# A fused graph and transformer layer on one core: seven blocks of normed tokens go through DRAM and are turned by VectorE

## The chip, the cores and the metric

The kernel runs on one core of a Trainium2 chip. A core has five engines that work side by side, each with its own list of instructions in a fixed order: TensorE (PE in the profile; its loading of weights is PEld), VectorE (DVE), ScalarE (ACT), GpSimd (POOL) and SyncE (SP), which here issues DMAs. They wait for each other through semaphores. Tiles lie in SBUF, a memory of 128 partitions; TensorE writes its products into PSUM; inputs, outputs and scratch tensors lie in DRAM and are moved by the core's 16 DMA engines. The metric is the device time of the whole kernel in microseconds, the median of several runs.

## The reference

4096 tokens of 256 values pass through one layer. First a graph part, then a transformer block on its normed result:

```python
x = x + gnn(layernorm(x), adj, neigh_W, lin_W)
x = x + ffn(layernorm(x))

def gnn(f, adj, neigh_W, lin_W):
    h = adj @ (f @ neigh_W.T) / (adj.sum(axis=1, keepdims=True) + 1.0)
    return concatenate([f, h], axis=-1) @ lin_W.T
```

`adj` is 4096 x 4096. The `ffn` is causal attention (4 heads for queries, 2 for keys and values, of 64 values, with rotary embedding) and a mixture of 8 experts of which each token uses 2. All is in float32.

## The kernel before

The tokens are cut into eight blocks of 512 (`NB`), a block into four tiles of 128 (`TB`). The kernel has three stages: the graph part with the making of queries, keys and values (to about 514 us), attention, and the experts. The change lies in the first.

The first stage makes eight passes, one for each block `b` of output tokens (`aggregate`, L510). A pass makes eight steps, one for each block `jb` of input tokens. A step multiplies one tile of adjacency of 1 MB, `a`, with the normed tokens `g[jb]`. It does so by seven products of halves instead of eight (Strassen's scheme), for which VectorE first makes four sums of parts of `a` (`halve`, L478: four instructions, L489 to L492, one of which writes into `a` itself). In TensorE's list a step has 28 instructions at L532. The order is written by hand: `aggregate` calls `halve` for the next step first, then the products, then a list of other work after the fourth of the seven products (`steps[jb]`), more at the step's end (`steps[jb, "end"]`), and then the load of the adjacency tile that is three steps ahead (`load`, L268). Three buffers hold adjacency, so this load can only start when the step's own tile has been read for the last time. All loads are issued on SP's queue, in the order of the program: a DMA that waits on SP holds back those behind it.

The other work of pass `b` is the making of queries, keys and values for block `b - 1` (`qkv`, L562), as one list for each step: in step 1 `scales` (statistics of the tokens) and `turn_tables` (VectorE turns the rotary tables, which lie along the other axis in DRAM, L311); in step 2 `norm` (VectorE writes the normed tokens `h0` into the buffers of this block's keys and values, L174) and `spread_tables` (three DMAs from SBUF to SBUF, L316); in step 3 `turn` (L582): TensorE turns `h0` so that channels lie on partitions, eight instructions with an identity matrix into PSUM (L431), and ScalarE copies the result to `qT[b]` in two instructions (L433); in step 4 `values_and_logits` (L589, with TensorE's L596) and the keys (`turned_heads`, L608, with TensorE's L612); in step 5 the queries. Rotation reads PSUM on VectorE (L619) and ScalarE (L621), and is ended by GpSimd (L625, L626). Block 7, the last, is not made by `qkv` but in the next stage.

`qT_all` holds the queries of all blocks, 1024 columns each. The columns of block `b + 1` are free while block `b` is being made, except for those of block 7, which hold sums of adjacency in this stage.

Of the kernel before, what the change touches and what calls it, by code (L numbers as in the profile page):

```python
# [9 lines left out]
F32 = mybir.dt.float32  # L10
# [3 lines left out]
ALU = mybir.AluOpType  # L14
# [3 lines left out]
P = 128  # L18
N = 4096
C = 256  # L20
# [46 lines left out]
def fast_kernel(  # L67
# [104 lines left out]
    def normed(dst, b, t, scale):  # L172

        nc.vector.tensor_scalar(  # L174
            dst, res[b][:, t, :], mv[b][:, t, 0:1], scale, op0=ALU.subtract, op1=ALU.mult
        )
# [8 lines left out]
        vv[NB - 1].rearrange("p (r t) c -> p r (t c)", r=2),  # L185
    ]
    m_late = qT_all[:, (NB - 1) * 1024 :][:, 0 : 2 * (C + 1)].rearrange("p (c o) -> p c o", c=2)

    def linear(pool, b, r, banks, m_sb):

# [16 lines left out]
    def ratio(pool, b):  # L207

        r = pool.tile([P, TB, 1], F32, tag="ratio", name=f"ratio_{b}", bufs=1)
        nc.vector.reciprocal(r, both[b])  # L210
        nc.vector.tensor_mul(r, r, rstd[b])
        return r
# [40 lines left out]
    with (  # L253
# [14 lines left out]
        def load(n):  # L268

            if n < NB * NB:  # L270
                blocks[n] = adjs.tile([P, TB, 512], F32, tag="a", name=f"a_{n // NB}_{n % NB}")
                nc.sync.dma_start(blocks[n], adj[n // NB, n % NB])
# [35 lines left out]
        def turn_tables(b):  # L308

            for k in range(2):  # L310
                nc.vector.transpose(tables[b][0:Q, k, :], tables[b][3 * Q :, k, :])  # L311

        def spread_tables(b):

            for n in range(1, 4):
                nc.sync.dma_start(tables[b][n * Q : (n + 1) * Q], tables[b][0:Q])  # L316
# [193 lines left out]
        def aggregate(b, steps):  # L510

            acc = [
                pool.tile([P, 2, 2 * P], F32, tag="acc", name=f"acc_{b}_{k}")
                for k, pool in enumerate((p_acc0, p_acc0, p_acc1, p_acc1))
            ]
            p = {number: acc[bank][:, at, :] for number, (bank, at) in AT.items()}

            u2 = u4 = neighbours[1][:, 0]
            u3 = neighbours[1][:, 1]
            for jb in range(NB):  # L520
                if b:
                    halve(b * NB + jb + 1)
                m = halves_of.pop(b * NB + jb)
                if jb == 0 and b:
                    load_tables(b - 1)
                for i, (number, left, right) in enumerate(
                    BY_BANK if jb in (0, NB - 1) else PRODUCTS
                ):
                    bank, at = AT[number]
                    for k in range(2):  # L530

                        nc.tensor.matmul(  # L532
                            acc[bank][:, at, :], g[jb][:, right, k, :], m[left][:, k, :],
                            start=(jb == 0 and k == 0 and at == 0),
                            stop=(jb == NB - 1 and k == 1),
                            skip_group_check=True,
                        )
                    if i == 3:
                        if jb == NB - 1:
                            nc.scalar.copy(u2, p[1])  # L540
                            nc.vector.tensor_add(neighbours[0][:, 0], u2, p[2])
                            nc.vector.tensor_add(u2, u2, p[6])
                            nc.vector.tensor_add(u3, u2, p[7])
                        for step in steps.get(jb, ()):
                            step()
                for step in steps.get((jb, "end"), ()):
                    step()
                load(b * NB + jb + 3)
            nc.vector.tensor_add(u4, u2, p[5])
            nc.vector.tensor_add(neighbours[1][:, 0], u4, p[3])  # L550
            nc.vector.tensor_sub(neighbours[0][:, 1], u3, p[4])
            nc.vector.tensor_add(neighbours[1][:, 1], u3, p[5])

        def turn_banks(b, r):
            return (
                p_pj.tile([P, 512], F32, tag="pj", name=f"ph_{b}_{r}"),
                p_tr.tile([P, 2, 2, P], F32, tag="tr", name=f"ph_{b}_{r}_1").rearrange(
                    "p c t i -> p (c t i)"
                ),
            )  # L560

        def qkv(b):  # L562

            made = {}

            def scales():
                stats(gx, b)
                var = mv[b][:, :, 1:2]
                power(both[b], var, *BOTH)
                power(rstd[b], var, 1.0, EPS_LN)  # L570

            def norm():

                made["h0"] = [
                    t.rearrange("p (t c) -> p t c", t=2)
                    for t in (kT[b], vv[b].rearrange("p t c -> p (t c)"))
                ]
                for t in range(TB):
                    normed(made["h0"][t // 2][:, t % 2, :], b, t, both[b][:, t])
                made["ratio"] = ratio(gx, b)  # L580

            def turn():  # L582

                made["hT"] = qT[b]
                transposed(
                    lambda t, c: made["h0"][t // 2][:, t % 2, c * P : (c + 1) * P], made["hT"]
                )

            def values_and_logits():  # L589
                for h in range(2):  # L590
                    pj = p_tr.tile([P, 2, 2, P], F32, tag="tr", name=f"pv_{b}_{h}")
                    pj = pj.rearrange("p c t i -> p c (t i)")
                    for i in range(2):
                        at = (2 * h + i) * P
                        for c in range(2):
                            nc.tensor.matmul(  # L596
                                pj[:, i, 0 : NE + P], made["hT"][:, c, at : at + P],
                                wqkv_sb[:, c, QK:], start=(c == 0), stop=(c == 1),
                            )
                    nc.scalar.copy(vv[b][:, 2 * h : 2 * h + 2, :], pj[:, :, NE : NE + P])  # L600
                    for i in range(2):
                        t = 2 * h + i
                        nc.scalar.activation(
                            first_lg[b][:, t, :], pj[:, i, 0:NE], AF.Copy,
                            scale=made["ratio"][:, t],
                        )

            def turned_heads(ms):  # L608
                pjs = [p_pj.tile([P, 512], F32, tag="pj", name=f"pq_{b}_{m}") for m in ms]
                for m, pj in zip(ms, pjs):  # L610
                    for c in range(2):
                        nc.tensor.matmul(  # L612
                            pj, wqkv_sb[:, c, m * P : (m + 1) * P], made["hT"][:, c, :],
                            start=(c == 0), stop=(c == 1),
                        )
                for m, pj in zip(ms, pjs):
                    to = kT[b] if m == 2 else qT[b][:, m, :]
                    rot = gx.tile([P, 512], F32, tag="rot", name=f"rot_{b}_{m}", bufs=1)
                    nc.vector.tensor_mul(to, pj, tables[b][:, 0, :])  # L619
                    for n in range(4):  # L620
                        nc.scalar.activation(  # L621
                            rot[n * Q : (n + 1) * Q, :], pj[(n ^ 1) * Q : ((n ^ 1) + 1) * Q, :],
                            AF.Copy, scale=1.0 if n % 2 else -1.0,
                        )
                    nc.gpsimd.tensor_mul(rot, rot, tables[b][:, 1, :])  # L625
                    nc.gpsimd.tensor_add(to, to, rot)  # L626

            return [
                [scales, lambda: turn_tables(b)], [norm, lambda: spread_tables(b)], [turn],
                [values_and_logits, lambda: turned_heads((2,))], [lambda: turned_heads((0, 1))],  # L630
            ]

# [37 lines left out]
        for b in range(NB):  # L672
            if b:

                steps = {0: behind, (0, "end"): at_end}
                behind = []
                for jb, fs in enumerate(qkv(b - 1)):
                    steps[jb + 1] = fs
            aggregate(b, steps)
            at_end = [lambda b=b: [linear(gx, b, r, turn_banks(b, r), m_sb) for r in range(2)]]  # L680
        nc.scalar.copy(m_late, m_sb)
# [4 lines left out]
    with (  # L686
# [201 lines left out]
            for p in range(2):  # L888
                nc.vector.tensor_mul(ys[b, p], ys[b, p], qT[b][:, p, :])


        def in_order(x):
            return x.rearrange("p (g c d) -> p c g d", g=4, c=2)

        def in_groups(x):
            return x.rearrange("p (c g d) -> p c g d", g=4, c=2)

        def inputs(b):

# [1077 lines left out]
        def step():  # L1977
            for f in next(rest, []):
                f()
# [802 lines left out]
```

## Time and profile before

| What | Number |
|---|---|
| Median of three runs | 1519.27 us (1518.95 to 1519.53) |
| The profiled execution, its own time | 1519.28 us |
| Its span, from the first to the last instruction | 1517.6 us |
| Granted TensorE clock, as a share of full speed | 0.999 |
| TensorE busy | 1504.7 us, 99% of the span |
| VectorE, ScalarE, GpSimd busy | 1071.6, 553.3, 564.8 us |
| One pass of the first stage | 59.70 us |
| One step of 28 products | 6.04 us |
| Adjacency loads, 1 MB each, from issue to landing | 64, median 4.9 us |

The share of busy time is an average over three stages. Where a step's work has to be ready, and what comes last there, is read from the chain of work that ended last and from the engines' timelines. In both, a line shows the start and the length in microseconds, the engine, the line of the kernel and the operation, what it writes and reads, and the count; in square brackets stands the idle time before it and what ended that. In the answers for single lines, the three numbers after the count are the shortest, median and longest duration in nanoseconds.

### The profile page before, as it was taken

How to read it: one execution, taken by the hardware profiler on the slowest of the kernel's cores; microseconds unless marked ns; L12 is line 12 of the kernel's file. 1: busy time of each engine (PE TensorE's matmuls, PEld its weight loads, DVE VectorE, ACT ScalarE, POOL GpSimd, SP SyncE). 2: the span in 40 equal slices, each digit the busy share in tenths (PEclk: the TensorE clock that was granted, in tenths of full speed). 3: DMA queues.
4: the chain of work that ended last, by engine and by line, in shares of the span. 5: the costliest groups of instructions: out<-in, count | busy, mean ns of one | idle time of the engine just before them, and what ended most of it. 6: DMA issues, size and time to landing. Idle time of an engine off the chain costs nothing.

```text
span 1517.6 us, 28636 instructions
## 1 busy us (share of the span) xinstructions
PE 1504.7 (99%) x10795; PEld 1109.5 (73%) x10795; DVE 1071.6 (71%) x2223; ACT 553.3 (36%) x991; POOL 564.8 (37%) x649
## 2 busy tenths in 40 slices
PE   9999999999999999999999999999999999999997
PEld 8888888888888643444444444348899999999996
DVE  7864655655756577778879879795676877777872
ACT  2102021121121356565655655653222344343341
POOL 2102122121220422364564553551523464554542
PEclk9999999999999999999999999999999999999999
DMA  6434544544434100001010111029977898999965
GB/s 243 132 121 149 175 143 131 171 143 149 154 138 152 36 2 16 29 33 52 33 43 31 43 44 31 29 67 330 259 188 214 257 268 243 268 267 247 274 155 134
DMA packets 105774, 212.19 MB, mean 140 GB/s; under 512 B 62394, under 2 KB 82106, under 8 KB 91994
## 3 DMA queue, kind: packets, MB, share of 16 engines
q1 hardware_dynamic: 92090, 192.00, 39.0%
q0 software_dynamic: 12720, 17.47, 6.4%
q8 instruction: 87, 1.43, 0.4%
q10 hardware_dynamic: 816, 0.79, 0.2%
q14 instruction: 61, 0.50, 0.1%
HBM read 184.48 MB, written 27.13 MB: 139 GB/s over the span
## 4 chain that ended last, share of the span: by engine, by line
PE 97%; DMA 1%; DVE 1%; POOL 0%; ACT 0%; issue 0%; SPq 0%; POOLq 0%; DVEq 0%
PE acc L532 25%; PE sc L785 15%; PE h L1793 13%; PE y_first L827 5%; PE y_second L827 5%; PE y_third L827 5%; PE ye_y L1847 4%; PE hA L1610 4%; PE ye_y L1750 3%; PE ye_ms L1750 3%; PE pq L612 2%; PE hD L1610 2%; PE pf L503 2%; PE ph L193 2%; PE po L913 1%; PE hB L1610 1%
## 5 line engine op out<-in xcount | busy, mean ns | idle before, releaser
L785 PE MATMUL sc<-qT_all,kT 64*64 64x512 f32 (+3 forms) x2304 | 282.1, 557 | 0.5 <-ACT pt_all L793 0.3
L532 PE MATMUL acc<-a,g 128*128 128x256 f32 x1024 | 244.0, 379 | 0.0
L532 PEld LDWEIGHTS acc<-a,g 128*128 128x128 f32 x1024 | 193.5, 190 | 31.8 <-issue 6.7
L785 PEld LDWEIGHTS sc<-qT_all,kT 64*64 64x64 f32 x2304 | 91.2, 133 | 128.6 <-issue 109.2
L793 ACT ACTIVATE pt_all<-sc 128x1024 f32<-128x1024 f32 (+3 forms) x157 | 148.8, 955 | 96.7 <-PE sc L785 94.2
L1873 POOL DMA_INDIRECT acc_dram<-y,late x40 | 63.3, 1583 | 176.9 <-ACT y L1862 113.5
L532 PE MATMUL acc<-more_sums,g 128*128 128x256 f32 x512 | 126.3, 379 | 0.0
L813 DVE TENSOR_TENSOR late<-late,pt_all 128x1024 f32<-128x1024 f32 (+3 forms) x91 | 106.8, 1174 | 24.3 <-POOL pt_all L795 9.9
L433 ACT COPY qT_all<-tr 128x512 f32<-128x512 f32 x30 | 16.3, 589 | 259.1 <-PE tr L431 259.1
L625 POOL TENSOR_TENSOR rot<-rot,tables 128x512 f32<-128x512 f32 x21 | 33.9, 1613 | 198.7 <-ACT rot L621 158.5
L532 PEld LDWEIGHTS acc<-more_sums,g 128*128 128x128 f32 x512 | 97.2, 190 | 13.2
L827 PE MATMUL y_first<-pt_all,vv 64*64 64x512 f32 (+3 forms) x448 | 106.6, 554 | 0.0
L1793 PE MATMUL h<-late,qT_all 128*128 128x256 f32 (+1 forms) x616 | 104.0, 327 | 0.2 <-DMA qT_all<-in_w_dram 0.2
L827 PE MATMUL y_second<-pt_all,vv 64*64 64x512 f32 (+3 forms) x436 | 104.2, 555 | 0.0
L1793 PEld LDWEIGHTS h<-late,qT_all 128*128 128x128 f32 x616 | 93.5, 191 | 9.9 <-ACT late L1477 1.1
L1075 POOL DMA_INDIRECT lists<-row,slots x64 | 88.4, 1381 | 17.3 <-issue 14.9
L827 PE MATMUL y_third<-pt_all,vv 64*64 64x512 f32 (+3 forms) x372 | 88.7, 555 | 0.0
L1800 DVE TENSOR_TENSOR late<-si,h 128x256 f32<-128x256 f32 (+2 forms) x87 | 39.4, 466 | 65.0 <-ACT si L1799 46.9
L621 ACT ACTIVATE rot<-pq 32x512 f32<-32x512 f32 x84 | 49.5, 589 | 82.6 <-DVE qT_all L619 43.6
L1799 ACT ACTIVATE si<-h 128x256 f32<-128x256 f32 (+2 forms) x87 | 36.0, 418 | 107.4 <-PE h L1793 98.5
L813 DVE TENSOR_TENSOR sum_all<-sum_all,pt_all 128x1024 f32<-128x1024 f32 (+3 forms) x51 | 56.0, 1098 | 15.8 <-POOL pt_all L795 9.5
L793 ACT ACTIVATE late<-sc 128x1024 f32<-128x1024 f32 (+3 forms) x55 | 50.9, 927 | 41.3 <-PE sc L785 37.9
(493 smaller groups left out, 3337.3 us busy)
## 6 DMA issues: line engine op xcount, KB each, us to landing
a<-in_adj_dram SPq DMA_DIRECT2D x64, 1024.0 KB, 4.9
qT_all<-in_w_dram SPq DMA_DIRECT2D x18, 1408.0 KB, 11.6
pt_all<-in_w_dram SPq DMA_DIRECT2D x16, 1408.0 KB, 10.8
res_all<-in_w_dram SPq DMA_DIRECT2D x17, 768.0 KB, 5.5
pt_all<-in_w_dram SPq DMA_DIRECT2D x16, 768.0 KB, 5.5
res_all<-in_w_dram SPq DMA_DIRECT2D x8, 1408.0 KB
qT_all<-in_w_dram SPq DMA_DIRECT2D x9, 768.0 KB, 5.4
late<-lists SPq DMA_DIRECT2D x96, 64.0 KB, 4.6
```

The lines of the kernel that those rows point to most:

```text
L532: nc.tensor.matmul(acc[bank][:, at, :], g[jb][:, right, k, :], m[left][:, k, :], start=(jb == 0 and k == 0 and at == 0), stop=(jb == NB - ...
L621: nc.scalar.activation(rot[n * Q : (n + 1) * Q, :], pj[(n ^ 1) * Q : ((n ^ 1) + 1) * Q, :], AF.Copy, scale=1.0 if n % 2 else -1.0,)
L785: nc.tensor.matmul(ps[k * HP : (k + 1) * HP, j, :w], kT[sb][hd, i * P + k * HP : i * P + (k + 1) * HP], qT[b][hd, p, off:], start=True, st ...
L793: nc.scalar.activation(pt[:, :, :w], ps[:, :, :w], AF.Exp, scale=HD ** -0.5)
L813: nc.vector.tensor_add(sums[b, p][:, :, off:], before[:, :, off:], pt[:, :, : 512 - off])
L827: nc.tensor.matmul(accs[b, p][k][hd, off:], vv[sb][some, i, hd], pt[some, j, : 512 - off], start=(s == order_of(b)[0]), stop=(s == order_o ...
L1075: put = nc.gpsimd.indirect_dma_start(out=lists[:, :], out_offset=bass.IndirectOffsetOnAxis(ap=chosen[b][:, k, t, :], axis=0), in_=flats[b] ...
L1610: nc.tensor.matmul(bank[:, n, :], m[left][:, c, :], m[right], start=first and n == 0, stop=True, skip_group_check=True,)
L1750: nc.tensor.matmul(p[number], m[left][:, j, :], m[right][:, j, :], start=(n % 4 == 0 and j == 0), stop=(j == 2), skip_group_check=True,)
L1793: nc.tensor.matmul(ps[m % 2][:, m // 2 - q, :], w13_sb[:, c, m * P : (m + 1) * P], xT[:, c, :], start=(c == 0), stop=(c == 1),)
L1847: nc.tensor.matmul(ps[h if last else 0][:, h, :], hT[:, q, cols], w2_sb[:, q, :], start=(q == 0), stop=(q == NF),)
L1873: put = nc.gpsimd.indirect_dma_start(out=(acc_dram if k < NM - LAST else out)[:, :], out_offset=at, in_=y[:, h, :], in_offset=None, comput ...
```

## The change

The seven blocks that `qkv` makes (0 to 6) are no longer turned by TensorE. `norm` writes the four groups of 32 channels of each head half in another order (`in_order`, `in_groups`, which were defined further down and are now above). `leave` stores the normed tokens in a scratch tensor in DRAM, `turning`, of which there are two for alternate blocks. `fetch` reads them back with four DMAs, each of which fills 32 partitions, in runs of 64 values, so that squares of 32 x 32 lie where they belong and only have to be turned in place; the target is `z`, in the columns of the next block in `qT_all`, or in a new tile `last_z` for block 6. `turn` is then two instructions of VectorE, one for each half of the channels.

The places move too. In step 2, `norm` is followed by `leave`; `fetch` stands at the end of step 2, ahead of the load of the adjacency of step 5; `spread_tables`, which followed `norm`, comes after this load, at a new place in the list called "loaded". `turn` moves from the middle of step 3 to its end. Step 3 has nothing in its middle.

```diff
@@ aggregate @@
                 for step in steps.get((jb, "end"), ()):
                     step()
                 load(b * NB + jb + 3)
+                for step in steps.get((jb, "loaded"), ()):
+                    step()
@@ before qkv @@
+        turning = [tc.dram_tile([512, C], F32, name=f"turning{n}") for n in range(2)]
+        last_z = gs.tile([P, 1024], F32, name="last_z")
@@ qkv, with in_order and in_groups @@
+    def in_order(x):
+        return x.rearrange("p (g c d) -> p c g d", g=4, c=2)
+    def in_groups(x):
+        return x.rearrange("p (c g d) -> p c g d", g=4, c=2)
...
                 for t in range(TB):
-                    normed(made["h0"][t // 2][:, t % 2, :], b, t, both[b][:, t])
+                    nc.vector.tensor_scalar(
+                        in_order(made["h0"][t // 2][:, t % 2, :]), in_groups(res[b][:, t, :]),
+                        mv[b][:, t, 0:1], both[b][:, t], op0=ALU.subtract, op1=ALU.mult,
+                    )
                 made["ratio"] = ratio(gx, b)
 
+            def leave():
+                for n, h0 in enumerate(made.pop("h0")):
+                    nc.sync.dma_start(
+                        turning[b % 2][n * 2 * P : (n + 1) * 2 * P].rearrange(
+                            "(t p) c -> p t c", p=P
+                        ),
+                        h0,
+                    )
+
+            def fetch():
+                made["z"] = qT_all[:, (b + 1) * 1024 : (b + 2) * 1024] if b + 2 < NB else last_z
+                squares = turning[b % 2].rearrange("(m i) (g e) -> g i m e", i=Q, g=4)
+                for n in range(4):
+                    nc.sync.dma_start(
+                        made["z"][n * Q : (n + 1) * Q].rearrange("p (m e) -> p m e", e=2 * Q),
+                        squares[n],
+                    )
+
             def turn():
                 made["hT"] = qT[b]
-                transposed(
-                    lambda t, c: made["h0"][t // 2][:, t % 2, c * P : (c + 1) * P], made["hT"]
-                )
+                z = made.pop("z").rearrange("p (m c d) -> p c m d", c=2, d=Q)
+                for c in range(2):
+                    nc.vector.transpose(
+                        qT[b][:, c, :].rearrange("p (m i) -> p m i", i=Q), z[:, c]
+                    )
...
             return [
-                [scales, lambda: turn_tables(b)], [norm, lambda: spread_tables(b)], [turn],
+                [scales, lambda: turn_tables(b)], [norm, leave], [],
                 [values_and_logits, lambda: turned_heads((2,))], [lambda: turned_heads((0, 1))],
-            ]
+            ], {
+                (2, "end"): [fetch], (2, "loaded"): [lambda: spread_tables(b)],
+                (3, "end"): [turn],
+            }
```

More of the change, by code (lines that the diff above doesn't have):

```diff
@@ L676, in fast_kernel @@
                 behind = []
-                for jb, fs in enumerate(qkv(b - 1)):
+                made_in, between = qkv(b - 1)
+                for jb, fs in enumerate(made_in):
                     steps[jb + 1] = fs
+                steps.update(between)
             aggregate(b, steps)
@@ L889, in normalize @@
                 nc.vector.tensor_mul(ys[b, p], ys[b, p], qT[b][:, p, :])
[L892 to L896, printed above, removed]
         def inputs(b):
```

## The prediction

> **What bounds the kernel now.** I read the page's busy table first, then the chain that ended last, in order of time, over the stage that the change touches, then the single rows that price its parts.
>
> ```profile
> PE 1504.7 (99%) x10795; PEld 1109.5 (73%) x10795; DVE 1071.6 (71%) x2223; ACT 553.3 (36%) x991; POOL 564.8 (37%) x649
> ...
> PE 97%; DMA 1%; DVE 1%; POOL 0%; ACT 0%; issue 0%; SPq 0%; POOLq 0%; DVEq 0%
> ```
>
> TensorE is busy 1504.7 of 1517.6 us and carries 97% of the chain, so what leaves TensorE's list shortens the end, as long as nothing else then comes late. The first stage (18 to 514 us) is eight passes over the adjacency. Its piece of the chain, for pass 1, which makes queries and keys of block 0:
>
> ```profile
> 105.56 15.54 PE acc L532 x72
> 121.10 0.87 PE tr L431 x8
> 121.98 6.04 PE acc L532 x28
> 128.02 1.85 PE pv L596 x16
> 129.87 1.72 PE pq L612 x4
> 131.59 6.04 PE acc L532 x28
> ```
>
> Start, length, what. There is no other engine in it: from 30 to 514 us every piece follows on the one before, with no wait. 72 products in 15.54 us are 0.216 us each, so the 28 of one tile of adjacency (one step jb) take 6.04 us. Step 1 ends at 111.60, step 2 at 117.64; step 3 runs 16 products, the eight transposes and 12 more products, to 124.56. Passes repeat every 59.70 us, and the transposes cost 0.87 us in each of seven.
>
> The rows below, from the answers on single lines and from VectorE's and SP's timelines, price the rest.
>
> ```profile
> L431 PE MATMUL tr<-ident,kT x28: 272/273/273, 120.9 to 479.5; 128*128 128x128 f32 x28
> ...
> L311 DVE STREAM_TRANSPOSE tables<-tables x14: 659/681/703, 111.1 to 470.0; 32x512 f32<-32x512 f32 x14
> ...
> L299 SPq DMA_DIRECT2D tables<-in_sin_dram x7: 481/481/487, 96.9 to 455.1; - x7
> ...
> L933 SPq DMA_DIRECT2D acc_dram<-res_all x8: 365/377/460, 626.9 to 1071.2; - x8
> ```
>
> Minimum, median and maximum in ns: one transpose shows 273 ns, but in the chain eight take 870, since they overlap; the chain's number is the one to use.
>
> ```profile
> 115.86 0.73 DVE L174 TENSOR_SCALAR vv<-res_all,mv,both 128x256 f32<-128x256 f32 x2
> ...
> 117.48 0.69 DVE L489 TENSOR_TENSOR qT_all<-a 128x512 f32<-128x512 f32 x1 [0.54 <-DMA a<-in_adj_dram]
> ...
> 122.60 0.69 DVE L489 TENSOR_TENSOR more_sums<-a 128x512 f32<-128x512 f32 x1 [2.30 <-DMA a<-in_adj_dram]
> ...
> 131.63 0.69 DVE L619 TENSOR_TENSOR kT<-pq,tables 128x512 f32<-128x512 f32 x1 [5.87 <-PE pq L612]
> ```
>
> ```profile
> 111.64 0.35 SPq L272 DMA_DIRECT2D a<-in_adj_dram  x1
> 112.47 1.94 SPq L316 DMA_DIRECT2D tables<-tables  x3
> 117.68 0.33 SPq L272 DMA_DIRECT2D a<-in_adj_dram  x1
> ```
>
> VectorE idles between 120.3 and 122.6 and between 125.8 and 131.6, and only waits for adjacency or for TensorE. SP sends each adjacency load the moment its buffer is free (111.64, 117.68) and idles otherwise.
>
> **What the skill says.** "DMA: Bandwidth & Descriptors", section "Why a DMA increments its semaphore by 16 and not by 1": a DMA runs on as many of the 16 engines as divide the slowest dimension of both its sides. The squares' loads have 32 on both sides, so 16. The trace agrees for the same shape: the 1024 packets of 128 B of the two tables (32x16x32) ran from 100.2 to 101.2 us at 13 ns each, which is 64 packets for each of 16 engines. Same page, "Why small descriptors are slow (HBM only)": a fixed cost per packet beside its bytes. The trace's packet records show it as 13 ns for 128 B, 27 for 512 B, 46 for 1 KB, 159 for 4 KB and 309 for 8 KB, about 0.037 ns per byte over a base of 8; so I estimate 18 ns for 256 B. Same page, "Anatomy of one DMA": some 2 us are fixed, most of it the receipt of the write. Here the 512 KB store of L933 lands 2.9 us after issue, with 0.91 us before its first packet and about 0.35 after its last; the measurement decides. "VectorE: DVE Perf Modes", "The three transpose paths": VectorE turns only 32x32 blocks, so the loads must bring the blocks to their places; L311 is the only case in this trace.
>
> **The change part by part**, for pass 1, by the clock above.
>
> Removed from TensorE: eight transposes, 0.87 us a pass. Seven passes (blocks 0 to 6) make 6.09 us. Removed from ScalarE: two copies L433 of 0.59 us, which nothing waits for but the removed path; no gain. Step 3 now ends at 124.56 - 0.87 = 123.69, and step 4's sixteenth product, after which values and logits (L596) read the turned tokens, at 123.69 + 3.45 = 127.14. That is the deadline of all that follows.
>
> Norm: the same four instructions with permuted patterns. L445, whose output is split in two runs, has a median of 406 ns and L174 407, so I cost the pattern at nothing. The second half is ready at 116.59.
>
> Store to DRAM, added: two DMAs of 256 KB, issued at about 116.0 and 116.65, nothing behind them on SP before 117.64. By L933: 0.91 to the first packet, 256 packets x 46 ns / 16 = 0.74, 0.35 to land: 118.7. The adjacency load ahead of it on the engines ended, by VectorE's wait, at 117.4 here and up to 0.8 us later in other passes, so I take 119.0.
>
> Fetch, added: it waits for both stores, and SP waits with it. Behind it stand the adjacency load of step 5, three table spreads and the load of step 6. Four issues at 0.37 to 0.60 us (L299, L882), by 0.48, are 1.9 us: SP is free at 120.9. First packet at 120.0; 2048 packets x 18 ns / 16 = 2.3 us; landed at 122.6.
>
> Turn, added: VectorE, after the halving for step 4 (done at 120.3) and ahead of the halving for step 5. Two STREAM_TRANSPOSE of 128x512; L311 has the same length over 32 partitions and takes 0.68, so 1.36: 122.6 to 124.0. Against 127.14 that is 3.1 us early. Cost on the path: nothing; step 4's first sixteen products cover it.
>
> Late next: the load of step 5 leaves at 120.9, not 117.68, and its 3.5 us of packets queue behind the fetch: landed at about 126.2 (before: 122.6). Its halving, 2.8 us in VectorE's idle stretch, ends at 129.0; step 5 starts at 123.69 + 6.04 + 1.85 + 1.72 = 133.30: 4.3 us early. The spreads, moved behind that load, need 96 packets x 159 ns / 16 = 1 us more: 127.2; L619 reads the tables at 130.76: 3.5 us early. The load of step 6 has its buffer at 123.69 and SP free at 123.2: not delayed at issue, landed at about 130.7, needed by 142.7. From there on each load again waits for TensorE alone, so no delay is carried into the next pass.
>
> Sum: -6.09 us. The profiled execution took 1519.28 (span 1517.6 and 1.7 around it), the median is 1519.27, so they can be exchanged: 1519.27 - 6.09 = 1513.2. After the stage everything hangs on TensorE's order and moves forward with it.
>
> Bounds of what the trace does not show. A 256 B packet lies between the 128 and 512 B rows, 13 to 27 ns: 1.7 to 3.5 us. A store lands after 2.1 to 2.9 us (L933's full size). A transpose over 128 partitions takes 0.66 to 1.76 us, the upper end being the longest VectorE instruction of that length in this stage (L492 at 144.17). All upper ends at once, with the late adjacency load: 120.3 + 0.95 + 3.5 + 0.35 + 3.5 = 128.6, a stall of 1.5 us, 0.6 more than was saved: +4.4 us in seven passes. With the transpose at L311's 0.68 the same sum is 126.5, no stall. A gain beyond 6.1 us has nothing to come from, since nothing else leaves TensorE.
>
> **The rivals.** First, a part of the gain is eaten: the round trip is one or two microseconds longer than each row says, and L596 waits up to 0.4 us a pass. Time 1513.6 to 1516. For it: two DMA trips in a row, and adjacency landings that scatter by 0.8 us. Against: 3.1 us of cover. Chance 0.05.
>
> Second, the wait takes the place of the transposes: the fetch lands near 126.6, the turn ends near 128.0 and L596 waits the 0.87 us that was saved; 1519.3, within 3 us either way. For it: a chip on which DRAM just written is slow to read, which this trace doesn't show. Chance 0.05.
>
> Third, slower: the fetch does not spread over the engines, because each of its four DMAs fills only 32 partitions. On four engines 2048 packets x 18 ns / 4 are 9.2 us: landed at 129.6, turned at 131.0, a stall of 3.8 and a net loss of 2.9 us a pass: 1540. It decides from a landing at 127.0 on (turn at 128.4, stall 1.3 = 0.87 + 3.0/7), which is fewer than about six engines. Against it stand the tables' packets, same shape, at 16. Chance 0.05.
>
> That TensorE still turned these blocks, so that the change did nothing, is excluded: its list of instructions has lost the 56 transposes.
>
> **How the numbers follow.** 0.85 for the forecast, whose own spread is what the runs of before scatter (0.6 us) and small waits: 1512.3 to 1514.5. About 0.2% (3 us) is what a measurement of this kernel can tell from no change. Faster: 0.85 + 0.05, less 0.01 of the first rival near its end: 0.89; same 0.06; slower 0.05. The range 1512.0 to 1516.0 holds the forecast and the first rival.
>
> **What would show it.** Right: TensorE without idle from 30 to 508 us, passes of 58.83 us, L596 released by nothing, the stage's end near 508; the fetch landing about 3.6 us after its first issue; VectorE waiting for it some 1 to 3 us before the turn; the load of step 5 issued 3 us after its buffer is free. Wrong: TensorE idle before L596 or before the first products of step 5, released by VectorE, or packets of 256 B much above 18 ns.

## The result, and the profile after

The changed kernel takes 1514.13 us (median of seven runs, 1513.33 to 1515.08) against 1519.27 (1518.81 to 1519.53): the ratio is 0.9967, with a 95% interval of 0.9955 to 0.9978. It is faster by 5.1 us; 6.09 were forecast. The profiled execution took 1513.40, with a span of 1511.7.

The busy table of the changed kernel (its line numbers are higher than before: the products are L538, the values L632, the turn L621):

```profile
PE 1498.3 (99%) x10739; PEld 1103.8 (73%) x10739; DVE 1082.8 (72%) x2237; ACT 545.3 (36%) x977; POOL 564.1 (37%) x649
```

TensorE has lost 56 instructions (10795 to 10739) and 6.4 us of busy time; VectorE has gained 14 and 11.2 us, ScalarE lost 14 and 8.0 us. TensorE's timeline in steps 3 to 5 of pass 1, the stretch that was shown of before (start, length, operation):

```profile
122.74 2.75 PE L538 MATMUL acc<-a,g 128*128 128x256 f32 x12
125.33 1.03 PE L538 MATMUL acc<-more_sums,g 128*128 128x256 f32 x4
126.19 1.03 PE L538 MATMUL acc<-qT_all,g 128*128 128x256 f32 x4
127.05 2.02 PE L632 MATMUL pv<-wqkv_sb,qT_all 128*128 128x136 f32 x16
```

The transposes are gone, and the values (L632) follow without idle time in brackets. When I set the start of every TensorE instruction beside its start in the kernel before, the distance grows by 0.87 us in each of the seven passes, at the place of the transposes and nowhere else. It is -0.07 us just before the first of them and 6.06 us at the end of the stage: the whole of the forecast.

SP and VectorE of the changed kernel around the fetch (SP: DMAs and their counts; VectorE: in brackets the idle time before and what ended it):

```profile
116.69 1.02 SPq L599 DMA_DIRECT2D turning<-vv  x1
119.54 1.96 SPq L611 DMA_DIRECT2D qT_all<-turning  x4
121.59 0.43 SPq L278 DMA_DIRECT2D a<-in_adj_dram  x1
122.07 1.89 SPq L322 DMA_DIRECT2D tables<-tables  x3
```

```profile
124.89 1.30 DVE L621 STREAM_TRANSPOSE qT_all<-qT_all 128x512 f32<-128x512 f32 x2 [5.13 <-DMA qT_all<-turning]
129.54 0.69 DVE L495 TENSOR_TENSOR more_sums<-a 128x512 f32<-128x512 f32 x1 [3.34 <-DMA a<-in_adj_dram]
...
131.68 0.68 DVE L498 TENSOR_TENSOR a<-a 128x512 f32<-128x512 f32 x1
```

The fetch starts at 119.54 (119.0 forecast) but its squares are ready only at 124.89 (122.6 forecast), so the turn begins 2.3 us later than I said, and the halving for step 5 at 129.54 instead of 126.2. Both are still in time. Measured as in the forecast, from the end of the second transpose (126.20) to the first of the values (127.05), the margin is 0.8 us in this pass and 1.4 to 2.6 in the other six, where 3.1 were forecast. The values' first weights need only the first transpose: in E5 below they are loaded 0.8 us after the turn's start. They are loaded at 126.84 here, so what is really left is 1.1 us in this pass and 1.6 to 2.9 in the others.

The halving is closer still. It ends at 132.36, and step 5 begins at 133.00: 0.6 us, where 4.3 were forecast. Over the seven passes it is between 2.9 us ahead and 0.5 us behind the start of step 5, and in pass 1 of E9 (below) 1.1 us behind. TensorE does not wait even then, because the first two of the seven products of a step read parts of `a` as they were loaded; the third, 1.7 us later, is the first to read a sum, and the sum that it reads was ready 1.2 us before it in that pass of E9.

So the stage gives all, and the end gives 5.1. One part goes at the start of attention. TensorE's first transposes of block 7 waited 0.39 us for VectorE before and wait 0.74 now. Here are VectorE's sums ahead of them and TensorE's wait, in the kernel before:

```profile
523.88 6.51 DVE L813 TENSOR_TENSOR late<-late,pt_all 128x1024 f32<-128x1024 f32 x5
...
530.78 0.44 PE L1161 MATMUL tr_l<-ident,h_l 128*128 128x128 f32 x2 [0.39 <-DVE h_l L174]
```

and in the changed kernel:

```profile
517.82 2.52 DVE L854 TENSOR_TENSOR late<-late,pt_all 128x1024 f32<-128x1024 f32 x2
520.79 3.89 DVE L854 TENSOR_TENSOR late<-late,pt_all 128x1024 f32<-128x1024 f32 x3 [0.46 <-DVE late L854]
...
525.06 0.65 PE L1196 MATMUL tr_l<-ident,h_l 128*128 128x128 f32 x3 [0.74 <-DVE h_l L174]
```

The five sums ran in one piece before; now there is a hole of 0.46 us after the second. GpSimd's small instruction on `rstd` (L165), which starts half a microsecond after the hole, also took 0.76 instead of 0.40 us. The hole costs 0.34 us; what makes it is taken up below, with E10.

### The profile page after: what moved, and what is told of

The parts are those of the page before. It is cut to its first block, busy times and chain, and to the rows that moved or that the text cites. A ratio compares the mean times of both kernels' runs of the same rounds, so it can differ in the third digit from the quotient of the medians.

```text
span 1511.7 us, 28589 instructions
## 1 busy us (share of the span) xinstructions
PE 1498.3 (99%) x10739; PEld 1103.8 (73%) x10739; DVE 1082.8 (72%) x2237; ACT 545.3 (36%) x977; POOL 564.1 (37%) x649
## 5 line engine op out<-in xcount | busy, mean ns | idle before, releaser
L538 PE MATMUL acc<-a,g 128*128 128x256 f32 x1024 | 244.0, 379 | 0.0
L538 PEld LDWEIGHTS acc<-a,g 128*128 128x128 f32 x1024 | 194.1, 190 | 32.1 <-issue 6.7
L538 PE MATMUL acc<-more_sums,g 128*128 128x256 f32 x512 | 126.3, 379 | 0.0
L538 PEld LDWEIGHTS acc<-more_sums,g 128*128 128x128 f32 x512 | 97.2, 190 | 13.1
L636 ACT COPY vv<-pv 128x256 f32<-128x256 f32 x14 | 5.2, 372 | 252.0 <-PE pv L632 144.1
```

The costliest lines, as they stand in the source:

```text
L538: nc.tensor.matmul(acc[bank][:, at, :], g[jb][:, right, k, :], m[left][:, k, :], start=(jb == 0 and k == 0 and at == 0), stop=(jb == NB - ...
```

## The experiments

**Once more, and where the rest went.** E1 is the changed kernel unchanged, for its scatter and a second trace; E2 takes away the only new wait that I could suspect.

> The changed kernel once more, for its scatter and a second trace. The profiled execution of the first look gained 5.9 us (6.09 forecast), but its median over seven runs is 1514.13, with runs from 1513.3 to 1515.1, where the kernel before has 1518.8 to 1519.5. Theory A (late turn): the fetch landed 2.2 us later than forecast, VectorE ended the turn only 0.6 to 2.4 us before TensorE wanted it, and in some executions one or more passes are late, so that TensorE waits before the values (L632 of the changed kernel). Theory B (elsewhere): the scatter has nothing to do with this wait; it comes from the added DMA traffic or from the start of attention, where the profile lost 0.34 us. Both expect a median near 1514.1 and a spread of 1.5 us or more; in a trace of a run above 1514.5, A expects TensorE to fall behind at L632, B elsewhere.

E1 measured a median of 1514.24 (1513.45 to 1515.06). Its trace is of a run of 1514.48, in the upper half of the scatter, and TensorE does not fall behind at L632 in it: the distance to before is again 6.05 us at the end of the stage, and 0.34 is lost at the start of attention. Another 0.60 us is lost where the experts begin. TensorE's wait for the first expert weights, in the kernel before, in the first trace of the changed one, and in E1:

```profile
1027.85 3.69 PE L1793 MATMUL h<-late,qT_all 128*128 128x256 f32 x16 [0.21 <-DMA qT_all<-in_w_dram]
```

```profile
1022.17 3.69 PE L1828 MATMUL h<-late,qT_all 128*128 128x256 f32 x16 [0.26 <-DMA qT_all<-in_w_dram]
```

```profile
1022.74 3.48 PE L1828 MATMUL h<-late,qT_all 128*128 128x256 f32 x15 [0.82 <-DMA qT_all<-in_w_dram]
```

It is a weight load that lands 0.6 us later in some executions, 510 us after the last fetch. Theory A finds no support: this trace shows no late turn (0.9 us are left in pass 1 by the measure of the forecast), and what was lost, was lost elsewhere (B), though not through the traffic (E4 below). Of the slowest runs, above 1515, there is no trace, so that a late turn in them is not excluded. The 25 runs of before that were timed beside this experiment lie between 1518.31 and 1520.51, as wide as those of the changed kernel; the narrow spread of the seven runs that I had first seen was small numbers.

```diff
@@ E2 @@
-                [values_and_logits, lambda: turned_heads((2,))], [lambda: turned_heads((0, 1))],
+                [], [lambda: turned_heads((0, 1))],
...
                 (3, "end"): [turn],
+                (4, "end"): [values_and_logits, lambda: turned_heads((2,))],
```

> The values, router products and keys move from the middle of step 4 to its end, so the turned tokens are wanted 2.6 us later; nothing else is moved. A: the wait can no longer occur, all runs come together at 1513.0 to 1513.6, the spread shrinks to that of before (0.7 us). B: as the changed kernel, median 1514.1, spread 1.5 us or more.

E2 measured 1513.58 (1513.38 to 1514.17), ratio 0.9962 with 0.9949 to 0.9976. The numbers are those that A expected, the narrower spread too (0.8 us against 1.6), but the trace does not show A's reason: the stage gained 6.01 us, as in the changed kernel, so there was no wait to remove in the runs that were traced. The difference is at the start of attention, where this trace has the 0.39 us of before.

**Is that 0.34 us chance?** The changed kernel and E2 once more, side by side.

> The changed kernel a third time, beside the next one, because five runs of each did not separate them. Both traces of the changed kernel so far gain 6.05 us in the first stage and lose 0.34 of it at the start of attention, where TensorE waits 0.74 instead of 0.39 us for VectorE's h_l. Theory E (that loss belongs to the kernel's timing): it is in this trace again, median 1514.0 to 1514.5. Theory F (chance of one execution): it is not, or of another size.

> The values at the end of step 4 once more. E: no loss at the start of attention, median 0.3 us or more below the changed kernel, 1513.4 to 1513.9. F: within 0.3 us of it.

E9 measured 1514.42 (1512.99 to 1514.84), ratio 0.9967 with 0.9955 to 0.9979; E10 1513.66 (1513.12 to 1513.86), ratio 0.9963 with 0.9950 to 0.9977. TensorE's wait and the sums in the trace of E9:

```profile
520.64 3.88 DVE L854 TENSOR_TENSOR late<-late,pt_all 128x1024 f32<-128x1024 f32 x3 [0.46 <-DVE late L854]
...
524.90 0.76 PE L1196 MATMUL tr_l<-ident,h_l 128*128 128x128 f32 x4 [0.74 <-DVE h_l L174]
```

and in the trace of E10:

```profile
517.75 6.51 DVE L855 TENSOR_TENSOR late<-late,pt_all 128x1024 f32<-128x1024 f32 x5
...
524.63 0.77 PE L1197 MATMUL tr_l<-ident,h_l 128*128 128x128 f32 x4 [0.39 <-DVE h_l L174]
```

Theory E stands in so far as the loss is no chance of one execution: the hole is in three of three traces of the changed kernel and in none of two of E2's. But it does not come from the shift in time. E3 (below), whose stage is only 0.8 us shorter than before, has the same hole and loses 0.35 us here; E2, shorter by 6.0, has none, nor has E5, which is longer by 5.8.

The traces give one more lead. The same hole stands elsewhere in kernels that lack it here: in the kernel before in pass 5, at the end of the norm, and in E2 and E5 in pass 3, between the first two instructions of a halving. TensorE does not wait for it there. The lines of the kernel before and of E2:

```profile
355.93 0.16 DVE L211 TENSOR_TENSOR ratio<-ratio,rstd 128x4 f32<-128x4 f32 x1 [0.46 <-DVE ratio L210]
```

```profile
266.51 0.69 DVE L496 TENSOR_TENSOR qT_all<-qT_all,a 128x512 f32<-128x512 f32 x1 [0.46 <-DVE qT_all L495]
```

In each of these traces, and in all four with the hole at the start of attention (the changed kernel's three and E3's), a DMA packet of 8 KB on a queue that the profile calls "instruction" starts 0.7 us after VectorE goes on. Where the five sums run in one piece in the traces of before, E2, E4, E5 and E10, no such packet starts until the last of them ends. So the hole may be a load of instructions for VectorE, whose place moves with the length of the lists, and a version loses 0.34 us or not by where it falls. This is not shown: the records do not say whose instructions they were, and other such packets have no hole before them, among them one during the sums in each of E6, E7 and E8.

E9 also loses 0.66 us at the first expert weights (a wait of 0.88); E2's two traces lose 0.3 and 0.5 there. With that the account closes as well as the scatter allows: 6.05 to 6.2 in the stage, less 0.34, less some 0.6 in two traces of three, is 5.1 to 5.7 where the experts begin, and 5.1 is the difference of the medians. Over all its runs, E2's version has a median of 1513.6 (ten runs, 1513.1 to 1514.2) and the changed kernel 1514.3 (eighteen, 1513.0 to 1515.1), so it is the best version found by its median, by 0.7 us, though the ranges overlap; 0.34 of these are explained.

**The place of the fetch.**

```diff
@@ E3 @@
-                (2, "end"): [fetch], (2, "loaded"): [lambda: spread_tables(b)],
+                (2, "loaded"): [fetch, lambda: spread_tables(b)],
```

> The fetch is issued behind the load of adjacency of step 5 instead of ahead of it. The load's 1 MB then takes its 3.5 us of the engines first: fetch packets from 122.2 to 125.4 (3.2 us as measured), landed at 126.5, turned at 127.8, wanted at 126.9. A: TensorE waits about 0.9 us in each of seven passes, which eats the gain: 1520, between 1517 and 1523. B (the turn's place is no limit): 1513 to 1515.

E3 measured 1518.87 (1516.98 to 1520.19), ratio 0.9993 with 0.9984 to 1.0001: the gain is nearly all gone. VectorE's turn and TensorE's values in pass 1 of E3:

```profile
126.65 1.30 DVE L621 STREAM_TRANSPOSE qT_all<-qT_all 128x512 f32<-128x512 f32 x2 [6.83 <-DMA qT_all<-turning]
```

```profile
127.51 2.39 PE L632 MATMUL pv<-wqkv_sb,qT_all 128*128 128x136 f32 x16 [0.24 <-DVE qT_all L621]
```

The squares land at 126.65, where I had put 126.5, because the load's packets run first; the values now wait for VectorE, and their second half for the second transpose. By the starts of TensorE's instructions these are 0.40 and 0.27 us in this pass (the brackets show less, because the ends of pipelined products are modelled). Putting the fetch in front of the load is worth the 4.6 us between this and the changed kernel. A's mechanism exists; in the changed kernel it is just not reached.

**The traffic by itself.** In E4 `norm` and `turn` are those of before, TensorE transposes in the middle of step 3, and the store, the fetch and the later spreads stay; what is fetched is not read.

```diff
@@ E4, against the changed kernel @@
-                    nc.vector.tensor_scalar(in_order(...), in_groups(...), ...)
+                    normed(made["h0"][t // 2][:, t % 2, :], b, t, both[b][:, t])
...
-                    nc.vector.transpose(...)
+                transposed(
+                    lambda t, c: made["h0"][t // 2][:, t % 2, c * P : (c + 1) * P], made["hT"]
+                )
...
-                [scales, lambda: turn_tables(b)], [norm, leave], [],
+                [scales, lambda: turn_tables(b)], [norm, leave], [turn],
...
-                (3, "end"): [turn],
```

> TensorE turns the blocks as before, in the middle of step 3; the store, the fetch and the later place of the table spreads stay, but nobody reads what was fetched. The traffic by itself: A expects the time and the spread of before, 1519.3 and 0.7 us, since no wait hangs on it; B expects 1520 or more and a spread of 1.5 us.

E4 measured 1519.48 (1518.46 to 1520.53), ratio 1.0000 with 0.9991 to 1.0008. Some 7 MB more of traffic, 42 more DMAs on SP and the later place of each pass's load of step 5 cost nothing that can be measured. Its spread is 2.1 us, as B expected, but so was that of before beside it (2.2 us), so the spread says nothing of the traffic. E4 leaves out the turn on VectorE; in the trace of E6 below, where VectorE turns six of the blocks as well, TensorE's starts in the stage do not fall behind before by more than the 0.1 us that it starts late.

**The cover taken away.**

```diff
@@ E5 @@
-                [values_and_logits, lambda: turned_heads((2,))], [lambda: turned_heads((0, 1))],
+                [], [lambda: turned_heads((0, 1))],
...
-                (3, "end"): [turn],
+                (3, "end"): [turn, values_and_logits, lambda: turned_heads((2,))],
```

> The values, router products and keys move to the end of step 3, directly behind the turn, so the sixteen products of step 4 no longer cover the round trip (3.45 us less). Theory A' (cover: what hides the round trip is exactly step 4's sixteen products): each pass waits for what is missing, 3.45 us minus the 0.6 to 2.4 us by which the turn was early in the traces (10.3 us over seven passes), so about 24.2 - 10.3 = 14 us are lost in all: 1528, between 1524 and 1531. Theory B' (the margin in the trace is not the margin of TensorE, other waits would cover it): 1514 to 1518.

E5 measured 1527.13 (1526.01 to 1528.65), ratio 1.0053 with 1.0037 to 1.0070: slower than before. TensorE in pass 1 of E5:

```profile
122.65 1.03 PE L538 MATMUL acc<-a,g 128*128 128x256 f32 x4
125.37 2.39 PE L632 MATMUL pv<-wqkv_sb,qT_all 128*128 128x136 f32 x16 [1.69 <-DVE qT_all L621]
```

The same two transposes that cost nothing in the changed kernel now hold TensorE for 1.69 us, and for 0.27 us more before the second. The loss against the changed kernel is 13 us (11.9 of them in the stage), 14 were expected. So step 4's sixteen products are what hides the round trip.

**Why the fetch landed late.** In E6 to E8 TensorE turns the blocks as in E4, and VectorE also turns the fetched squares of blocks 0 to 5, into columns of `qT_all` or `last_z` that nobody reads. Only the source of the fetch differs: E6 reads the squares of `turning`, E7 squares of the input `x`, E8 `turning` in runs of 4 KB. In E7 and E8 what comes back is not the turned tokens; it is not used. In E7 SP has no store to wait for.

```diff
@@ E7, against E6 @@
-                squares = turning[b % 2].rearrange("(m i) (g e) -> g i m e", i=Q, g=4)
+                squares = x[b * 512 : (b + 1) * 512].rearrange("(m i) (g e) -> g i m e", i=Q, g=4)
@@ E8, against E6 @@
-                squares = turning[b % 2].rearrange("(m i) (g e) -> g i m e", i=Q, g=4)
+                rows = turning[b % 2].rearrange("(n i m) e -> n i m e", n=4, i=Q)
...
-                        made["z"][n * Q : (n + 1) * Q].rearrange("p (m e) -> p m e", e=2 * Q),
-                        squares[n],
+                        made["z"][n * Q : (n + 1) * Q].rearrange("p (m e) -> p m e", e=C),
+                        rows[n],
```

> TensorE turns the blocks, and VectorE turns the fetched squares too, into columns that nobody reads (blocks 0 to 5), so that its wait shows the landing of the fetch while no result hangs on it. Time 1519 to 1520. From the first issue of the fetch to the turn: 5.3 us if, as in the changed kernel, it is the cost of this transfer.

> As the last one, but the squares are read from the input x instead of from the tensor that has just been written; what is fetched is not used. Theory C (DRAM just written is slow to read): from the first issue to the turn 3.6 us, the forecast. Theory D (the price is that of 2048 small runs and of their landing): 5 us or more.

> As e6, but the same 512 KB come back in runs of 4 KB (128 packets) from the tensor just written; what is fetched is not used. C: as e6, about 5 us. D: four issues of 0.5 us, 128 packets x 159 ns / 16 = 1.3 us, which fit inside the issues, 0.95 ahead and 0.35 behind: 3.5 us.

The times of these single runs are 1519.74, 1520.97 and 1519.83. The turn in pass 1 of E6, then of E7, then of E8, each with SP's fetch where it differs:

```profile
124.66 1.30 DVE L627 STREAM_TRANSPOSE qT_all<-qT_all 128x512 f32<-128x512 f32 x2 [4.84 <-DMA qT_all<-turning]
```

```profile
117.88 2.12 SPq L608 DMA_DIRECT2D qT_all<-in_x_dram  x4
...
123.47 1.31 DVE L627 STREAM_TRANSPOSE qT_all<-qT_all 128x512 f32<-128x512 f32 x2 [3.67 <-DMA qT_all<-in_x_dram]
```

```profile
119.11 1.73 SPq L608 DMA_DIRECT2D qT_all<-turning  x4
...
123.42 1.30 DVE L627 STREAM_TRANSPOSE qT_all<-qT_all 128x512 f32<-128x512 f32 x2 [3.37 <-DMA qT_all<-turning]
```

From first issue to turn E6 needs 5.1 us in this pass (4.7 to 5.4 over six), E7 5.6 (5.4 to 6.2), E8 4.3 (4.1 to 4.9). Theory C falls: squares from an input that nobody wrote come no sooner, and the packets of 256 B take no less time (20.6 ns on average in E7, 20.0 in E6). They come later in E7, where the fetch does not pause for the store. The store hardly shares the engines with it (its last packet ends 0.14 us after the fetch's first starts, in pass 1); the load of adjacency that follows 1.5 us sooner does, with packets from 121.57 on, while the fetch's last packet ends at 122.95. How much of the delay this makes is not shown. D's direction holds, but with a small part of the size: runs sixteen times as long bring 0.8 us, not 1.6. The records of DMA packets in the first trace divide pass 1 of the changed kernel: 0.98 us to the first packet, 3.20 us of packets (120.52 to 123.72) and 1.17 us from the last packet to the turn. Over all passes the third part lies between 0.3 and 1.2 us; in E8 it is 0.96 us in pass 1 and 0.45 to 1.03 in all, so it does not belong to the small runs. The 1 MB loads of adjacency of the kernel before have 0.4 us in that place when nothing stands behind them on the queue, but 0.75 to 1.06 in the four passes that show it for the load followed by the three table spreads. So it may belong to what follows on the queue and not to these four DMAs; no run separates the two.

## Why the prediction was right, and where it was off

The step that decides, eight transposes at 0.87 us in seven passes, held: 6.06 us at the stage's end against 6.09. That they could be priced from the chain, since TensorE has no idle time in the stage, held too; so did the two transposes (1.30 against 1.36 us), the costless norm, SP free after the last fetch (121.5 against 120.9), and "no delay is carried into the next pass": each pass gained the same. E4 and the trace of E6 confirm that what was added lies under other work, and E5 names the work.

Four terms were mis-sized. The fetch's way: of the 3.6 us from first issue to landing, the 0.95 to the first packet were right (0.98), the packets took 3.2 and not 2.3 us, and the landing 1.2 and not 0.35. The packet of 256 B had been put at 18 ns, which is the median; the sum over the packets, shared by 16 engines, is 2.65 us, or 21 ns each, and the engines did not end together. Hence a cover of 0.8 to 2.6 us, where the text says 3.1. The bounds given there, 13 to 27 ns and 1.7 to 3.5 us, did hold the packets, but I gave the landing no bound at all and took it from the store of L933, a transfer of other shape.

These bounds were not needed. The text calls L311 the only transpose of VectorE in the trace and the packet of 256 B one that the trace does not show; neither is so. The experts of the kernel before already fetch squares (L1441, into 32 partitions in runs of 256 B) and turn them on VectorE (L1490). The page of before has such a fetch, with its time from issue to landing:

```profile
late<-lists SPq DMA_DIRECT2D x96, 64.0 KB, 4.6
```

The 33280 packets of L1441 have a median of 18 ns and an average of 23, and the 24 transposes of L1490 with 512 columns over 128 partitions take 0.70 us on average. By the average the packets of the fetch would have been put at 2.9 us, and a single DMA half as large that takes 4.6 us, if in a stage with more traffic, speaks against four that land after 3.6.

The load of step 5 was forecast to land at 126.2 and landed at 129.5. Part of this is the later issue (121.6 against 120.9) and the later fetch before it; the load of step 6, issued at 124.06, then runs beside it. The 4.3 us of slack shrank to as little as -1.1 us, as told above. That this cost nothing is luck as far as the forecast goes: it counted on the sums being ready before step 5 starts and said nothing of which product reads them first.

"After the stage everything hangs on TensorE's order and moves forward with it" failed in the size of 0.34 us: in the changed kernel VectorE's sums have a hole at the start of attention, and TensorE waits for them there. The step had no row behind it; the wait of 0.39 us, 16 us after the stage, was in the trace of before and was not read.

The forecast's own spread was put at 1512.3 to 1514.5 from the scatter of three runs. The median lies in it, but single runs go to 1515.1, and before itself to 1520.5. The first weights of the experts, waited for by 0.2 to 1.8 us (the last in E7), are one place where executions differ.

Of the rivals, the first (a part eaten by late squares) did not occur, although its premise did: the squares were late by more than two microseconds, and the cover was enough. The second and the third were not seen; the fetch spread over the engines as forecast, for 2048 packets of 21 ns on average in 3.2 us need at least 13 of them at once. The rival that I lacked is a small wait far down that changes from version to version, though nothing was changed there.

## What to carry to other kernels

Work can leave a saturated TensorE by a long way round, store, fetch and turn, if the reader stands far enough behind: count from the issue of the data's first step to the instruction that reads it, and see what TensorE does in between (here 3.45 us of products, worth 13 us when taken away). Where a small transfer and a large one share a queue, the one with the nearer deadline goes first; the order alone was worth 4.6 us here. When a gain is smaller at the end than in its stage, set both traces beside each other instruction by instruction: the point where the distance jumps names the wait. Before a transfer is priced by interpolation, search the whole trace for one of the same shape, and take the average of its packets and its time to landing, not the commonest packet.

## What the runs showed of the hardware

Four DMAs of 128 KB, each into 32 partitions in runs of 256 B, took 4.1 to 5.4 us from first issue until VectorE could read them; the same bytes in runs of 4 KB took 4.1 to 4.9. Of this 0.3 to 1.2 us lie after the last packet, against 0.4 for a load of 1 MB with nothing behind it and 0.75 to 1.06 for one with the table spreads behind it. A STREAM_TRANSPOSE over 128 partitions costs what one over 32 costs: 0.69 against 0.68 us for 512 columns. The traces of before, of the changed kernel and of E2, E3 and E5 each have a hole of 0.46 us between two instructions of VectorE that no other engine ends, and 0.7 us after it a packet on an instruction queue; whether the packet makes the hole is not shown.
